# Pair 1's attention scores in a second buffer, half of their masking moved earlier, and four weight sums moved between engines

## The chip, the cores and the metric

The kernel runs on one core of a Trainium2 chip. The metric is the device time of one execution in microseconds (us). A core has five engines with a queue each: TensorE (PE; its weight loads are shown as PEld), VectorE (DVE), ScalarE (ACT), GpSimd (POOL) and SyncE (SP), which here only issues transfers (DMA).

## The reference

128 graphs of 128 nodes, with 512 features per node in fp32, go through two layers. Each layer's output is added to its input and normalised. Cut to what is computed:

```python
# layer 0: graph attention, 8 heads of 64 units
feats = einsum('bnf,hfu->bhnu', X, W)
dense = e_self[..., :, None] + e_neigh[..., None, :]   # two dot products per node and head
dense = leaky_relu(dense, 0.2) + -1e10 * (1 - A)
out   = softmax(dense) @ feats + b                      # heads side by side: 512 features
x = layernorm(x + relu(out))
# layer 1: two hypergraph convolutions over the same adjacency matrix
# conv(x) = D^-1 H B^-1 H^T (x @ W^T) + b
h = relu(conv(x; W1, b1))                               # 512 -> 1024
h = layer_norm(h) * gamma + beta
y = conv(h; W2, b2) + x                                 # 1024 -> 512
x = layernorm(x + y)
```

## The kernel before

**Pairs.** Two graphs are worked on together: 64 pairs, numbered p. A work step is a small function of a pair (for instance `masked`, line 586, which adds the mask to 128 x 512 scores on POOL). Each step has a lag and a time, and its due time is (p + lag) x T + time with T = 38.6. The list `todo` (lines 1140 to 1161) holds the steps done once, chiefly the preparation of the weights, with their due times; the dict `first` (lines 1163 to 1188) overrides due times for the first pairs, since the weights aren't ready then. At the end everything is sorted by due time and called in that order under a manual schedule. A due time is thus only a rank: it decides where in each engine's queue the instructions stand. Each engine runs its queue strictly in order, and semaphores make an instruction wait for its operands and for the buffer that it writes.

**Matrix products.** The large products use a scheme of seven half-size products in place of eight (numbers 1, 2, 6, 5, 7, 4, 3 in the order of issue). `chain` (line 326) makes the steps of one such product: seven products into PSUM banks named X, Y and W, and copies of X to SBUF by ACT between them. pf are the features of the attention, ph the products of the first convolution, py those of the second; pz is the product of y with the propagator R = D^-1 H B^-1 H^T. The scheme needs sums of blocks of the operands: `x_sums` (line 474, xS), `z_sums` (836, zS) and `h_sums` on POOL for the moving data, and sums of the weights, which are done once. For W1 they are s1 to s4, each 128 x 1024 elements (`prepare_hidden`, lines 243 to 249); for W2 t1 to t4 (`second_sums`, lines 222 to 226, by way of `prepare_output_block_sums`, 305). Before that, `prepare_output_blocks` (295) folds gamma into W2's blocks.

**Attention of a pair.** `features` by the chain pf, then f_sum (503) on DVE joins the products; `spread_rows` (537) transposes the node terms and writes them to DRAM (rd) by a DMA of SP, and `neighbours` (559) reads them back broadcast over all partitions into the tile nb, two DMAs of 512 KB, one for each graph of the pair. Then, for each graph g and half i of the heads: `masked` (586, POOL), `leaky` (593, ACT), `largest` (607, DVE, row maximum nm), `exponential` (616, ACT). `e_write` and `e_read` (621 to 634, SP) send the exponentials through DRAM, and `e_transpose` (636, DVE) turns blocks of them into eT, which `attend_pair` (692, PE) multiplies with the features. `add_bias` (741, POOL) adds the bias to the features, `residual` (751, DVE) adds x, `rstds` (764, POOL) takes the reciprocal root of the variance (rsa), ACT scales (line 796) to give y. The first pairs 0 and 1 get their features by plain products (L523).

**Other steps named here.** `edges` (412 to 429, DVE) makes the transposed incidence matrix hT and its degrees, `scale_edges` (431, DVE) divides by them; `x_transpose` (382, DVE) gives xT; `h_sum` (865, DVE), `relu` (876, ACT), `square` (890, ACT) and `squares` (902, POOL) make the hidden layer and its mean square; `skip` (803, DVE) adds y and bias into the output tile o. `mask` (376, POOL) makes the tile neg.

**Buffers.** Tiles are allocated from a pool by tag; the same tag is the same memory, and a new tile of the tag waits for the readers of the old one. nb has one buffer. The tag sq, of the same size, holds the squares of the hidden layer from pair 0's on, and before that a raw block of layer 0's weights; the tag xS also serves early temporaries.

Of the kernel before, what the change touches and what calls it, by code (L numbers as in the profile page):

```python
# [8 lines left out]
F32 = mybir.dt.float32  # L9
AF = mybir.ActivationFunctionType  # L10
# [10 lines left out]
def kernel(  # L21
# [45 lines left out]
    nc = tc.nc  # L67
    G, N, F = x.shape
    P = 128
    DH = w1t.shape[1]  # L70
    H = 8
    U = F // H
    KF = F // P
# [10 lines left out]
    work = ctx.enter_context(tc.tile_pool(name="work", bufs=1))  # L84
# [4 lines left out]
    def bank(name):  # L89
        return psum.tile([P, HALF], F32, tag="bank", name=name)  # L90
# [106 lines left out]
    w1_sb = const.tile([P, 7, KF // 2, HALF], F32, name="w1_sb")  # L197
    w1_21 = work.tile([P, KF // 2, HALF], F32, tag="h", name="w1_21")
# [6 lines left out]
    ident = const.tile([P, P], F32, name="ident")  # L205
# [5 lines left out]
    for i in range(2):  # L211
        t = const.tile([P, 2, H, UW + 1], F32, name=f"ft{i}")
# [37 lines left out]

    gbs = const.tile([P, KH, 2], F32, name="gbs")
    made = {}

    def prepare_vectors():
        t = bank("vecs_T")
        nc.tensor.transpose(t[:, :3 * KH], vec_rows, ident[:3 * KH, :3 * KH])
        nc.scalar.copy(vecs.rearrange("p v k -> p (v k)"), t[:, :3 * KH])
# [58 lines left out]
    def step(lag, time, since=0, until=PAIRS):  # L316

        def keep(fn):
            steps.append((lag, time, fn.__name__, range(since, until), fn, ()))
            return fn  # L320
        return keep
# [236 lines left out]

    @step(1, 27.0)
    def neighbours(p, s):  # L560
        s["nb"] = work.tile([P, 2, H * N], F32, tag="nb", name=f"nb_{p}")
        for g in range(2):
            dst, src, hs = s["nb"][:, g, :], s["rd"], slice((2 + g) * H, (3 + g) * H)
            if p == 0:
                src = src[hs].rearrange("h b j -> (h b j)")
            else:
                dst = dst.rearrange("p (b x) -> p b x", b=NB)
                src = src[:, hs, :].rearrange("b h j -> b (h j)")
            queue = nc.scalar if p == 0 and g == 1 else nc.sync
            queue.dma_start(dst, src.partition_broadcast(P))  # L570
# [553 lines left out]
    for t, fn, *args in (  # L1124
# [21 lines left out]
        (15.46, load_weights, (nc.sync, w1_blocks[:1:-1], w1t, F // 2, HALF)),  # L1146
        (16.1, everywhere, (b2_bc, b2, nc.sync)),
        (79.0, prepare_hidden, (nc.gpsimd, 0)), (79.1, prepare_hidden, (nc.gpsimd, 1)),
        (120.7, prepare_hidden, (nc.gpsimd, 2)), (110.6, prepare_hidden, (nc.vector, 3)),
        (15.5, prepare_output_vectors, ()), (16.0, prepare_output, ()),  # L1150
        (78.3, prepare_rows, ()), (78.79, prepare_output_sums, ()),
        (78.99, prepare_output_spread, (0, "gw")), (98.0, prepare_output_spread, (1, "bw")),
        (98.1, prepare_output_bias, ()), (98.2, prepare_output_blocks, (slice(0, 1),)),
        (99.75, prepare_output_blocks, (slice(1, 2),)),
        (117.8, prepare_output_blocks, (slice(2, 3),)),
        (118.1, prepare_output_blocks, (slice(3, 4),)),
        (126.5, prepare_output_block_sums, (nc.gpsimd, slice(0, 2))),
        (126.57, prepare_output_block_sums, (nc.vector, slice(2, 3))),
        (141.0, prepare_output_block_sums, (nc.vector, slice(3, 4))),
        (100.0, prepare_mean_columns, ()),  # L1160
    ]

    first = {
        ("spread_rows", 0): 13.5, ("neighbours", 0): 14.0,
        ("nodes", 0): 12.9, ("write_nodes", 0): 12.92, ("spread_nodes", 0): 15.9,
        ("edges", 0): 14.46, ("edges", 2): 119.2,
        ("x_transpose", 2, 0): 120.5, ("x_transpose", 2, 1): 121.1, ("scale_edges", 0): 14.47, ("propagator", 0): 14.55,
        ("r_evict", 0): 97.845,
        ("spread_rows", 1): 15.72, ("nodes", 1): 15.55, ("write_nodes", 1): 15.85,
        ("edges", 1): 110.4, ("scale_edges", 1): 110.5, ("neighbours", 1): 80.1,  # L1170
        ("propagator", 1): 121.7, ("spread_nodes", 1): 80.3, ("r_evict", 1): 121.8,
        ("leaky", 0, 1, 1): 77.65, ("leaky", 0, 0, 1): 73.6, ("largest", 0, 0, 1): 75.3,
        ("attend", 0, 0, 0): 78.95, ("attend", 0, 0, 1): 78.96, ("attend", 0, 1, 0): 78.97,
        ("attend", 0, 1, 1): 78.98, ("attended", 0, 0): 97.8, ("attended", 0, 1): 97.82,
        ("add_bias", 0, 0): 13.6, ("add_bias", 0, 1): 13.61,
        ("residual", 0, 0): 97.81, ("residual", 0, 1): 97.83, ("rstds", 0, "a"): 97.84,
        ("leaky", 1, 0, 0): 113.0, ("leaky", 1, 0, 1): 117.9, ("leaky", 1, 1, 0): 119.9,
        ("largest", 1, 0, 0): 113.1, ("largest", 1, 0, 1): 118.2, ("largest", 1, 1, 0): 120.2,
        ("masked", 1, 0, 0): 98.0, ("masked", 1, 0, 1): 98.1, ("masked", 1, 1, 0): 98.2, ("masked", 1, 1, 1): 120.65,
        ("exponential", 1, 0, 0): 119.85, ("exponential", 1, 1, 1): 126.6,  # L1180
        ("square", 0, 0, 0): 134.5, ("square", 0, 0, 1): 134.6,
        ("mask", 3): 152.0, ("sum_blocks", 0): 149.75, ("write_sums", 0): 149.76,
        ("read_sums", 0): 149.77,
# [96 lines left out]
```

## Time and profile before

| | |
|---|---|
| time, median of 3 runs (lowest to highest) | 2387.93 us (2385.42 to 2389.12) |
| the profiled execution's own time | 2389.21 us |
| its span from first to last instruction | 2387.4 us |
| granted TensorE clock, mean | 0.998 |
| PE busy | 2357.5 us, 99% |
| DVE busy | 2089.5 us, 88% |
| POOL busy | 1824.8 us, 76% |
| ACT busy | 1528.3 us, 64% |
| DMA | 347.09 MB, 145 GB/s over the span |

Durations below come from the profiled execution. A timeline row gives start and duration in us, engine, line, operation, output and inputs with their shapes, a count, and, in brackets, the idle time of the engine before it with what released it. "L249" is line 249 of the kernel. A row with a count of more than one covers adjacent instructions.

### The profile page before, as it was taken

The page shows a single profiled execution, that of the slowest core. Times are in us where ns is not written, and L with a number is a line of the kernel's source. Part 1 is how long each engine was busy: PE and PEld are TensorE (multiplying, and loading weights), DVE is VectorE, ACT ScalarE, POOL GpSimd, SP SyncE. Part 2 cuts the span into 40 slices and gives each one's busy share as a digit, 9 for nine tenths or more (in the row PEclk, how much of TensorE's full clock was granted, in tenths as well). Part 3 has the DMA queues.
Part 4 walks back from the last instruction along what each step waited for, and adds up shares of the span by engine and source line. Part 5 has one row for each costly group of instructions (what it writes and reads, how often), then busy time and mean ns, then how long its engine had stood idle before and what let it go on. Part 6 is the DMA issues. An engine that isn't in the chain of part 4 may idle for free.

```text
span 2387.4 us, 80667 instructions
## 1 busy us (share of the span) xinstructions
PE 2357.5 (99%) x32309; PEld 1941.2 (81%) x32309; DVE 2089.5 (88%) x4456; ACT 1528.3 (64%) x4481; POOL 1824.8 (76%) x2060
## 2 busy tenths in 40 slices
PE   7999999999999999999999999999999999999998
PEld 5777887878878888888888888888888887888886
DVE  7989888889898898898898988988988989889886
ACT  4565766766756667667667666666576676666763
POOL 5877787787777877877877878778778777787784
PEclk9999999999999999999999999999999999999999
DMA  6545555555545545455555545545555555455431
GB/s 198 137 144 147 150 150 137 154 150 143 155 144 149 149 149 145 148 150 150 142 148 153 148 142 156 150 144 144 148 148 149 147 141 149 144 148 152 146 118 50
DMA packets 431134, 347.09 MB, mean 145 GB/s; under 512 B 151440, under 2 KB 380328, under 8 KB 430760
## 3 DMA queue, kind: packets, MB, share of 16 engines
q1 hardware_dynamic: 427288, 337.46, 49.7%
q8 instruction: 256, 4.19, 0.7%
q10 hardware_dynamic: 3472, 4.47, 0.6%
q14 instruction: 118, 0.97, 0.2%
HBM read 239.08 MB, written 102.73 MB: 143 GB/s over the span
## 4 chain that ended last, share of the span: by engine, by line
PE 91%; DMA 3%; DVE 3%; ACT 1%; issue 1%; SPq 1%; POOL 0%; DVEq 0%; POOLq 0%; ACTq 0%
PE phX L97 18%; PE pyX L97 17%; PE phW L97 9%; PE pfX L97 9%; PE pyW L97 8%; PE phY L97 4%; PE pfW L97 4%; PE pq L97 4%; PE pav L705 4%; PE pz L97 4%; PE pyY L97 4%; PE pfY L97 2%; DMA nb<-rd 1%; PE pd L97 1%; DMA rd<-rows 1%; PE pf L523 1%
## 5 line engine op out<-in xcount | busy, mean ns | idle before, releaser
L344 ACT COPY py<-pyX 128x257 f32<-128x257 f32 x189 | 70.6, 374 | 529.3 <-PE pyX L97 445.6
L97 PEld LDWEIGHTS phX<-zS,w_sb 128*64 128x64 f32 x6144 | 347.7, 137 | 37.4 <-POOL ft L744 22.8
L97 PE MATMUL phX<-zS,w_sb 128*64 128x128 f32 x6144 | 370.7, 273 | 2.6 <-ACT ph L344 2.6
L906 POOL TENSOR_TENSOR sq<-sq 128x512 f32<-128x512 f32 (+2 forms) x384 | 343.2, 894 | 20.1
L589 POOL TENSOR_TENSOR nb<-nb,neg 128x512 f32<-128x512 f32 x256 | 319.8, 1281 | 29.5 <-DMA nb<-rd 26.5
L605 ACT ACTIVATE nb<-nb,ft 128x128 f32<-128x128 f32 x1020 | 325.1, 392 | 16.7 <-POOL nb L589 16.4
L619 ACT ACTIVATE nb<-nb,nm 128x128 f32<-128x128 f32 x1024 | 319.4, 391 | 4.7 <-DVE nm L611 4.7
L769 POOL TENSOR_TENSOR rso<-veo,mhalf 128x2 f32<-128x2 f32 x63 | 44.1, 700 | 337.4 <-DVE veo L767 337.4
L97 PE MATMUL pyX<-w_sb,h 128*64 128x257 f32 x2016 | 241.8, 379 | 0.5 <-ACT py L344 0.5
L97 PE MATMUL pyX<-w_sb,hS 128*64 128x257 f32 x2016 | 241.9, 379 | 0.0
L97 PE MATMUL pyW<-w_sb,hS 128*64 128x256 f32 x2016 | 241.2, 379 | 0.1
L883 ACT ACTIVATE h<-h,vecs 128x128 f32<-128x128 f32 x768 | 239.7, 393 | 1.9 <-DVE h L868 1.1
L611 DVE TENSOR_REDUCE nm<-nb 128x4 f32<-128x512 f32 x256 | 175.2, 684 | 50.5 <-ACT nb L605 42.2
L744 POOL TENSOR_TENSOR ft<-ft,b_bc 128x512 f32<-128x512 f32 x128 | 203.9, 1612 | 6.0 <-ACT ft L533 6.0
L97 PEld LDWEIGHTS pyX<-w_sb,h 128*64 128x64 f32 x2016 | 158.5, 136 | 61.4 <-ACT py L344 0.9
L97 PEld LDWEIGHTS pyW<-w_sb,hS 128*64 128x64 f32 x2016 | 158.1, 136 | 60.4 <-issue 0.7
L97 PEld LDWEIGHTS pyX<-w_sb,hS 128*64 128x64 f32 x2016 | 151.9, 136 | 53.1
L640 DVE STREAM_TRANSPOSE eT<-eb 128x512 f32<-128x512 f32 x252 | 163.5, 685 | 4.5 <-DMA eb<-ed 3.6
L807 DVE SCALAR_TENSOR_TENSOR o<-y,b_bc 128x512 f32<-128x512 f32 x128 | 166.7, 1341 | 0.0
L894 ACT ACTIVATE sq<-h 128x512 f32<-128x512 f32 x256 | 160.8, 629 | 2.1
L1008 DVE SCALAR_TENSOR_TENSOR y<-y,rsh,bw_bc 128x512 f32<-128x512 f32 x126 | 148.1, 1213 | 15.7 <-POOL rsh L1004 15.7
L469 POOL TENSOR_TENSOR hS<-h 128x512 f32<-128x512 f32 x126 | 161.8, 1284 | 0.0
(178 smaller groups left out, 5603.9 us busy)
## 6 DMA issues: line engine op xcount, KB each, us to landing
nb<-rd SPq DMA_DIRECT2D x127, 512.0 KB, 5.9
ed<-nb SPq DMA_DIRECT2D x126, 512.0 KB, 2.7
eb<-ed SPq DMA_DIRECT2D x504, 128.0 KB, 2.9
x<-in_x_dram SPq DMA_DIRECT2D x64, 512.0 KB, 4.1
out_dram<-o SPq DMA_DIRECT2D x63, 512.0 KB, 3.7
xb<-in_x_dram SPq DMA_DIRECT2D x248, 128.0 KB, 3.0
a<-in_adj_dram SPq DMA_DIRECT2D x64, 128.0 KB
w<-in_adj_dram SPq DMA_DIRECT2D x128, 64.0 KB, 4.0
```

The lines of the kernel that those rows point to most:

```text
L97: nc.tensor.matmul(to[rows], lhs[:, rows], rhs, start=start, stop=stop, skip_group_check=True)
L469: engine.tensor_tensor(t[:, i], in0, in1, op=op)
L589: nc.gpsimd.tensor_tensor(t, t, neg[:, :, None, :].to_broadcast([P, NB, HH, B]), op=ALU.add)
L605: nc.scalar.activation(t, t, AF.Prelu, bias=s["ft"][:, g, h, 0:1], alpha=SLOPE)
L611: nc.vector.tensor_reduce(s["nm"][:, g, hs], scores(p, s, g, hs).rearrange("p b h j -> p h b j"), AX.XY, ALU.max, negate=True,)
L619: nc.scalar.activation(t, t, AF.Exp, bias=s["nm"][:, g, h:h + 1])
L640: nc.vector.transpose(s["eT"][:, g, hs, :].rearrange("p h (b i) -> p h b i", b=NB), s["eb", g][:, :, hs, :].rearrange("p b h j -> p h b j"),)
L744: nc.gpsimd.tensor_tensor(t, t, b0_bc.rearrange("p (h u) -> p h u", h=H), op=ALU.add)
L807: nc.vector.scalar_tensor_tensor(s["o"][:, g, :], s["y"][:, g, :], 2.0, b2_bc, op0=ALU.mult, op1=ALU.add)
L883: nc.scalar.activation(dst[:, k, :], src[:, k, :], AF.Relu, bias=b1_sb[:, c:c + 1])
L894: nc.scalar.activation(s["sq"][:, g, q * KH // 2:(q + 1) * KH // 2, :], hid(s, g, q), AF.Square, scale=DH ** -0.5,)
L906: nc.gpsimd.tensor_tensor(t[:, :n, :], t[:, :n, :], t[:, n:2 * n, :], op=ALU.add)
```

## The change

Four things are changed, all in the first pairs and in the preparation of weights.

- The scores of pair 1 get a tile of the tag sq in place of nb, and the step `neighbours` of pair 1 is due at 16.15 and not 80.1: in SP's queue its two DMAs now stand ahead of loads for pair 2 (xb, a, w).
- `masked`, `leaky`, `largest` and `exponential` of pair 1 get new due times. Two of its four masks stand on POOL before the weight sum s2, the other two ahead of s4; the first two leaky steps stand on ACT before pair 0's y is scaled.
- The weight sum s3 = a11 - w1_21 leaves POOL: PE multiplies a11 by the identity and w1_21 by minus the identity into the same PSUM bank, for two blocks of 512 columns (four products of 128 x 512), and ACT copies the two banks to SBUF. s4, t3 and t4 leave DVE for POOL.
- Steps around them are reordered: edges(1), edges(2), x_transpose(2), e_transpose(1, 1) and the blocks of W2. From pair 3 on the order of every engine's instructions is unchanged.

```diff
--- before.py
+++ after.py
@@ -251,6 +251,21 @@
     gbs = const.tile([P, KH, 2], F32, name="gbs")
     made = {}
 
+    def prepare_minus():
+        made["minus"] = work.tile([P, P], F32, tag="xS", name="minus")
+        nc.scalar.activation(made["minus"], ident, AF.Identity, scale=-1.0)
+
+    def prepare_hidden_banks():
+        made["s3"] = [bank(f"s3_{k}") for k in range(KF // 2)]
+
+    def prepare_hidden_products():
+        for k, t in enumerate(made["s3"]):
+            nc.tensor.matmul(t, ident, w1_sb[:, 0, k, :], start=True, stop=False)
+            nc.tensor.matmul(t, made["minus"], w1_21[:, k, :], start=False, stop=True)
+
+    def prepare_hidden_out(k):
+        nc.scalar.copy(w1_sb[:, 5, k, :], made["s3"][k])
+
     def prepare_vectors():
         t = bank("vecs_T")
         nc.tensor.transpose(t[:, :3 * KH], vec_rows, ident[:3 * KH, :3 * KH])
@@ -558,7 +573,9 @@
 
     @step(1, 27.0)
     def neighbours(p, s):
-        s["nb"] = work.tile([P, 2, H * N], F32, tag="nb", name=f"nb_{p}")
+        s["nb"] = work.tile(
+            [P, 2, H * N], F32, tag="sq" if p == 1 else "nb", name=f"nb_{p}"
+        )
         for g in range(2):
             dst, src, hs = s["nb"][:, g, :], s["rd"], slice((2 + g) * H, (3 + g) * H)
             if p == 0:
@@ -1146,38 +1163,65 @@
         (15.46, load_weights, (nc.sync, w1_blocks[:1:-1], w1t, F // 2, HALF)),
         (16.1, everywhere, (b2_bc, b2, nc.sync)),
         (79.0, prepare_hidden, (nc.gpsimd, 0)), (79.1, prepare_hidden, (nc.gpsimd, 1)),
-        (120.7, prepare_hidden, (nc.gpsimd, 2)), (110.6, prepare_hidden, (nc.vector, 3)),
+        (98.2, prepare_hidden, (nc.gpsimd, 3)), (15.52, prepare_minus, ()),
+        (78.985, prepare_hidden_banks, ()), (98.05, prepare_hidden_products, ()),
+        (110.35, prepare_hidden_out, (0,)), (119.95, prepare_hidden_out, (1,)),
         (15.5, prepare_output_vectors, ()), (16.0, prepare_output, ()),
         (78.3, prepare_rows, ()), (78.79, prepare_output_sums, ()),
         (78.99, prepare_output_spread, (0, "gw")), (98.0, prepare_output_spread, (1, "bw")),
         (98.1, prepare_output_bias, ()), (98.2, prepare_output_blocks, (slice(0, 1),)),
-        (99.75, prepare_output_blocks, (slice(1, 2),)),
-        (117.8, prepare_output_blocks, (slice(2, 3),)),
-        (118.1, prepare_output_blocks, (slice(3, 4),)),
-        (126.5, prepare_output_block_sums, (nc.gpsimd, slice(0, 2))),
-        (126.57, prepare_output_block_sums, (nc.vector, slice(2, 3))),
-        (141.0, prepare_output_block_sums, (nc.vector, slice(3, 4))),
+        (98.25, prepare_output_blocks, (slice(1, 2),)),
+        (99.0, prepare_output_blocks, (slice(2, 3),)),
+        (99.1, prepare_output_blocks, (slice(3, 4),)),
+        (120.65, prepare_output_block_sums, (nc.gpsimd, slice(0, 1))),
+        (126.5, prepare_output_block_sums, (nc.gpsimd, slice(1, 2))),
+        (126.57, prepare_output_block_sums, (nc.gpsimd, slice(2, 3))),
+        (139.3, prepare_output_block_sums, (nc.gpsimd, slice(3, 4))),
         (100.0, prepare_mean_columns, ()),
     ]
 
     first = {
+        ("e_transpose", 1, 1, 1): 132.48,
+        ("e_transpose", 1, 1, 0): 132.47,
+        ("edges", 2): 126.58,
+        ("x_transpose", 2, 1): 117.95,
+        ("x_transpose", 2, 0): 117.9,
+        ("scale_edges", 1): 98.6,
+        ("edges", 1): 98.5,
+        ("exponential", 1, 1, 1): 126.52,
+        ("exponential", 1, 1, 0): 121.95,
+        ("exponential", 1, 0, 1): 119.9,
+        ("exponential", 1, 0, 0): 119.85,
+        ("largest", 1, 1, 1): 121.9,
+        ("largest", 1, 1, 0): 117.86,
+        ("largest", 1, 0, 1): 98.31,
+        ("largest", 1, 0, 0): 98.3,
+        ("leaky", 1, 1, 1): 121.8,
+        ("leaky", 1, 1, 0): 117.85,
+        ("leaky", 1, 0, 1): 79.08,
+        ("leaky", 1, 0, 0): 79.06,
+        ("masked", 1, 1, 1): 98.1,
+        ("masked", 1, 1, 0): 98.0,
+        ("masked", 1, 0, 1): 79.07,
+        ("masked", 1, 0, 0): 79.05,
+        ("neighbours", 1): 16.15,
         ("spread_rows", 0): 13.5, ("neighbours", 0): 14.0,
         ("nodes", 0): 12.9, ("write_nodes", 0): 12.92, ("spread_nodes", 0): 15.9,
-        ("edges", 0): 14.46, ("edges", 2): 119.2,
-        ("x_transpose", 2, 0): 120.5, ("x_transpose", 2, 1): 121.1, ("scale_edges", 0): 14.47, ("propagator", 0): 14.55,
+        ("edges", 0): 14.46, 
+        ("scale_edges", 0): 14.47, ("propagator", 0): 14.55,
         ("r_evict", 0): 97.845,
         ("spread_rows", 1): 15.72, ("nodes", 1): 15.55, ("write_nodes", 1): 15.85,
-        ("edges", 1): 110.4, ("scale_edges", 1): 110.5, ("neighbours", 1): 80.1,
+        
         ("propagator", 1): 121.7, ("spread_nodes", 1): 80.3, ("r_evict", 1): 121.8,
         ("leaky", 0, 1, 1): 77.65, ("leaky", 0, 0, 1): 73.6, ("largest", 0, 0, 1): 75.3,
         ("attend", 0, 0, 0): 78.95, ("attend", 0, 0, 1): 78.96, ("attend", 0, 1, 0): 78.97,
         ("attend", 0, 1, 1): 78.98, ("attended", 0, 0): 97.8, ("attended", 0, 1): 97.82,
         ("add_bias", 0, 0): 13.6, ("add_bias", 0, 1): 13.61,
         ("residual", 0, 0): 97.81, ("residual", 0, 1): 97.83, ("rstds", 0, "a"): 97.84,
-        ("leaky", 1, 0, 0): 113.0, ("leaky", 1, 0, 1): 117.9, ("leaky", 1, 1, 0): 119.9,
-        ("largest", 1, 0, 0): 113.1, ("largest", 1, 0, 1): 118.2, ("largest", 1, 1, 0): 120.2,
-        ("masked", 1, 0, 0): 98.0, ("masked", 1, 0, 1): 98.1, ("masked", 1, 1, 0): 98.2, ("masked", 1, 1, 1): 120.65,
-        ("exponential", 1, 0, 0): 119.85, ("exponential", 1, 1, 1): 126.6,
+        
+        
+        
+        
         ("square", 0, 0, 0): 134.5, ("square", 0, 0, 1): 134.6,
         ("mask", 3): 152.0, ("sum_blocks", 0): 149.75, ("write_sums", 0): 149.76,
         ("read_sums", 0): 149.77,
```

## The prediction

> **What bounds the kernel now.** First the page's busy shares, then a table of stretches, to see where PE stands idle:
>
> ```profile
> PE 2357.5 (99%) x32309; PEld 1941.2 (81%) x32309; DVE 2089.5 (88%) x4456; ACT 1528.3 (64%) x4481; POOL 1824.8 (76%) x2060
> ```
>
> Stretches (us; busy and count of PE, PEld, DVE, ACT, POOL; clock; DMA share; GB/s):
>
> ```profile
> 40.00:44.00 4.00, 3.16 (x30) 1.34 (x26) 3.76 (x10) 0.58 (x1) 0.92 (x1) 1.00 0.95 174
> 44.00:48.00 4.00, 0.57 (x6) 0.57 (x8) 3.90 (x12) 2.01 (x6) 2.55 (x3) 0.55 0.51 167
> 48.00:52.00 4.00, 4.00 (x48) 4.00 (x46) 3.90 (x13) 2.68 (x9) 2.50 (x7) 0.60 0.32 56
> 60.00:100.00 40.00, 34.98 (x479) 28.84 (x476) 38.83 (x74) 22.88 (x69) 34.80 (x35) 1.00 0.54 124
> 100.00:132.00 32.00, 29.77 (x376) 22.58 (x374) 28.14 (x63) 17.67 (x52) 21.95 (x22) 1.00 0.54 156
> 132.00:200.00 68.00, 68.00 (x946) 53.95 (x948) 60.38 (x129) 43.45 (x129) 52.20 (x61) 1.00 0.50 146
> 300.00:1000.00 700.00, 699.68 (x9700) 569.15 (x9698) 620.90 (x1328) 453.46 (x1333) 546.53 (x615) 1.00 0.52 148
> ```
>
> From 132 us PE is full; the change moves nothing there. So only the fill can pay. In it the timeline has these PE gaps: 4.27 before pz, 0.69, 0.26, 0.67 and 0.48 at 61 to 70, 0.92 at 90.54, 1.91 at 96.16, 0.34 at 116.22, 1.89 at 131.88: 11.4 us, 0.48% of the span, is all that closing gaps can win. To it comes a clock of 0.55 to 0.60 at 44 to 52, in which pz took 3.68 us where later ones take 1.75 to 1.94. Meanwhile DVE is 94 to 98% busy: in the fill it is the second bound.
>
> The timeline rows that the change touches (start, us, engine, line; the bracket is idle time before and its releaser):
>
> ```profile
> 36.11 2.37 POOL L249 TENSOR_TENSOR w_sb<-w,w_sb 128x1024 f32<-128x1024 f32 x1 [2.67 <-DMA w<-in_w1t_dram]
> 39.38 1.22 SPq L570 DMA_DIRECT2D nb<-rd  x2
> ...
> 45.45 0.71 POOL L769 TENSOR_TENSOR rsa<-vea,mhalf 128x2 f32<-128x2 f32 x1 [4.52 <-DVE vea L767]
> ...
> 47.43 3.68 PE L97 MATMUL pz<-R,y 128*64 128x128 f32 x32 [4.27 <-ACT y L796]
> ...
> 50.63 1.22 DVE L249 TENSOR_TENSOR w_sb<-w_sb 128x1024 f32<-128x1024 f32 x1
> ...
> 63.19 1.37 DVE L226 TENSOR_TENSOR w_sb<-w_sb,w 128x1024 f32<-128x1024 f32 x1
> ...
> 68.13 4.79 DVE L807 SCALAR_TENSOR_TENSOR o<-y,b_bc 128x512 f32<-128x512 f32 x2
> ...
> 75.58 2.15 DVE L226 TENSOR_TENSOR w_sb<-w_sb 128x1024 f32<-128x1024 f32 x1
> ...
> 96.16 1.97 PE L97 MATMUL phX<-zS,w_sb 128*64 128x128 f32 x32 [1.91 <-ACT ph L344]
> ```
>
> POOL stands idle for 4.52 us before rsa; three weight sums (1.22, 1.37, 2.15) sit in DVE's full queue. The chain of waits ends the fill with a transfer:
>
> ```profile
> 117.54 4.28 DMA rd<-rows
> 121.83 2.96 DMA nb<-rd
> 124.79 2.55 issue
> 131.88 1.97 PE phX L97 x32
> ```
>
> [...] 2.37 on POOL against 1.22 on DVE for one 128x1024 sum. [...] the two skips take 4.79 beside POOL's sums (L807's mean is 1.69 over the fill) and a residual (L753) 0.66 to 1.81. [...] the gaps of 1.9 halved nothing.
>
> **The change, part by part.** Sums are against the profiled execution: 2389.21 us with a span of 2387.4, 1.8 around it, 1.3 above the median of 2387.93.
>
> *Second buffer and early load.* Pair 1's scores waited for pair 0's nb, read by PE's transposes until 38.7. In a tile tagged sq they wait for rd's write, landed at 36.3. The two nb DMAs now stand before xb x4, a and w x2 of pair 2 on SP; those seven issue after the wait, 3 us later, and serve work at 51 us and beyond: nothing. The load itself: issue 36.3, landing 3.0 later (nb at 121.83 in the chain) to 6.2 (230.67 there, busier queues), so 39.3 to 42.5; I take 41, as the DMA share is 0.98 at 36 to 40.
>
> *POOL.* After s1 (ends 38.48) it runs two masks (1.28 each), s2 (2.37), and then rsa: 2.56 + 2.37 = 4.93, ending at 45.9 with the landing at 41. That is about when y needs rsa, since y is late too: its two residuals (0.90 and 0.69 at 40.57 and 43.52) had POOL mostly idle and now run beside masks. L753's spread, 0.66 to 1.81, bounds it at 0.0 to 1.1 each; I take 1.1 together, so pz begins at 48.5 instead of 47.43. Behind rsa stand two more masks and s4, 2.56 + 2.37 from 46.6, then the memsets and neg (0.6): zS starts at 52.1 where it started at 51.83. The phX that reads it, at 54.45, is where it was, perhaps 0.3 late. t1 takes the place of s3 at 55.94 (2.37 both within 0.3), t2 and t3 stand where t1 and t2 stood; so t4 is what POOL gains. It comes before the squares at 78.83, and POOL has no gap from 61.25 to 91: its 2.2 to 2.7 would push rsa at 84.77 and pz at 87.24, had not xS and hS come earlier by about as much (xT, which xS waited 2.94 for, is moved ahead of edges(2), 2.4 us). Nothing; cover gone, up to 2.4 on pz.
>
> *PE.* s3 becomes four 128x512 products in the gap before pz. No row has that shape; two passes of 2x512 took 1.12 (gw), so 0.56 each at the least; the 128x264 product of L523 takes 0.45, so 0.87 for 512. I take 0.87: 3.5 in a gap of 4.27, so they end at 46.7. Operands late, they would push pz one for one, up to 3.5. PE is then idle for 1.8 and not 4.27 before pz, so the clock stays full: pz takes 1.85 and not 3.68. pz's end: 48.5 + 1.85 = 50.35 against 51.11; the next phX is at about 50.4 against 50.90, -0.5 (bounds -1.7 with unhindered residuals, +1.3 if the clock halves all the same). But at 54.45 zS decides, as worked out under POOL: of the -0.5 **0.0** is left (up to +0.3). ACT's two copies (0.58 each) and minus (0.39) fall in its idle time at 39.3 to 43.2 and in queues that PE doesn't wait for until 61: nothing, up to 0.6 on the gap at 61.09.
>
> *DVE up to 74.* s4 (1.22) and t3 (1.37) leave. edges(2), with its degree 2.4 us in all, moves from 56.09 to about 62, behind an h_sum, and its scale_edges follows: 2.4 - 1.37 = +1.0 before the h_sum of (1,0) at 66.31, 1.9 if the small DVE operations there, now beside add_bias and t2, wait once more. Its relus hold up the pf copy: pfX at 70.22 comes +1.0 to +1.9, I take **+1.4**. Then eT(1,1) twice (1.29) precedes the skips and the f_sum that frees pfW at 73.76; pfW is already 1.4 late by pfX, and the skips and f_sum have that much slack from it: nothing more (bounds 0 to 1.3).
>
> *DVE from 75 to 100.* t4 is gone: -2.15 at 75.58 on a full DVE, which feeds rden, y and the largest of pair 2: 1.4 - 2.15 = -0.75 there, which the gap of 0.92 can take, and the gap of 1.91, which waits on ACT behind an exp and DVE's largest, as well. At 100: **-1.0** (bounds -2.8, both gaps, to +1.4, neither).
>
> *The last gap.* rd's issue at 117.54 follows the rows transposed at 117.09 and SP's own ab issues (to 117.44); 4.28 + 2.96 + 2.55 behind it don't shrink. The rows come after pair 2's products and would be earlier by 1.0, SP's queue, with its own waits for DMAs and POOL, only in part: a third is kept. Sum at 132: **-0.3** (-2.8 to +1.7). 2387.93 - 0.3 = 2387.6.
>
> **Rivals.** A, the gaps close: 0.69 + 0.26 + 0.67 + 0.48 = 2.1 and 0.92 + 1.91 = 2.83 are won, and rd starts as much earlier. With 0.5 kept from pz, -5.4: 2382.5. For it: DVE loses 4.74 us in a stretch where it is the bound. Against: edges and eT move into the very stretch, and the last gap takes back. B, slower: nb lands late. POOL stands at the first mask, and s2, rsa, y and pz stand behind it. Free until 41 to 41.5; from there one for one. If it lands at 45.9, as its second half did before, rsa is at 45.9 + 4.93 = 50.8, +5.4, pz runs at half clock again, of which no later step has to give back more than the 0.3 of the forecast: +5.1, 2393. For it: a DMA share of 0.95 to 0.98 at 36 to 44; against: 3 us earlier issue, ahead of xb. C, no win from the clock or t4: s3 leaves PE idle enough that pz runs at half rate, phX +1.3, and DVE's +1.4 at 70 isn't given back, as t4 on POOL holds up rsa: +1 to +2, 2389.5. D, it is all hidden: the transfer at 117.54 starts when it did, 2387.9, inside the forecast.
>
> **How the numbers follow.** Forecast with D, 0.71 (own range 2385.5 to 2389.7); C 0.12; A 0.10; B 0.07. A change under 0.2% (4.8 us) is about what can't be told from none here: three runs spread over 3.7. Faster takes most of A: 0.09; slower takes B and a tail of C: 0.08; same 0.83. The range leaves out B and most of A: 2384.0 to 2390.8.
>
> **What would show it.** nb landing and POOL's first L589 of pair 1 at 41 or sooner; four short PE rows between 43 and 47; clock 1.00 at 44 to 52 and pz near 1.85; rsa within 1 us of 45.5; pfX at 71 and pfW at 74 to 75; the gaps at 90 and 96 smaller; PE's phX after the last gap near 131.6 and the same busy PE afterwards. Wrong if POOL waits for nb past 42, if pz stays at 3.68, or if anything after 132 has changed.

## The result and the profile after

| | before | after |
|---|---|---|
| time, median of 20 runs each (lowest to highest) | 2387.91 us (2385.29 to 2389.94) | 2391.31 us (2388.61 to 2393.98) |
| ratio to before, 95% interval | | 1.0015 (1.0008 to 1.0022) |
| span of the profiled execution | 2387.4 us | 2390.7 us |
| third pair's first phX (the "last gap" ends) | 131.88 us | 135.55 us |
| the next 20 pairs | 729.33 us | 731.31 us |
| the 41 pairs after those | 1488.60 us | 1486.28 us |

Slower by 3.4 us. The last three rows come from the starts of phX in the two traces, one execution each. They show two losses: 3.7 us in the fill and 2.0 in pairs whose instructions the change doesn't touch. (The 2.3 that after wins at the end is a disturbance at 1938 to 1957 us in the profiled execution of before, with PE gaps of 0.62 and 1.26.) Such rows compare kernels only roughly: the runs of one kernel spread over 5 us or so, and one early product (pf of pair 0's second graph) starts anywhere from 19.9 to 21.5 us in the fourteen traces, 1.1 us earlier in after than in before.

The table of stretches, after (us; busy and count of PE, PEld, DVE, ACT, POOL; clock; DMA share; GB/s):

```profile
40.00:44.00 4.00, 4.00 (x8) 1.53 (x9) 3.79 (x9) 1.00 (x4) 2.30 (x2) 0.78 1.01 197
44.00:48.00 4.00, 3.73 (x7) 1.25 (x5) 3.93 (x12) 2.45 (x9) 4.00 (x4) 0.79 1.05 142
48.00:52.00 4.00, 3.08 (x56) 3.03 (x58) 3.90 (x10) 3.69 (x8) 4.00 (x3) 1.00 0.45 81
60.00:100.00 40.00, 33.30 (x412) 26.78 (x410) 30.26 (x68) 19.98 (x59) 30.98 (x30) 0.91 0.43 106
100.00:132.00 32.00, 31.92 (x418) 24.93 (x416) 29.14 (x67) 16.99 (x49) 21.55 (x23) 1.00 0.60 156
```

The clock is full where pz runs now, as intended, but it is at 0.91 in 60 to 100, where it was 1.00, and DVE is busy for 30.26 of those 40 us where it was busy for 38.83. The timeline shows where both come from:

```profile
66.91 1.73 SPq L648 DMA_DIRECT2D eb<-ed  x4
...
71.55 1.30 DVE L657 STREAM_TRANSPOSE eT<-eb 128x512 f32<-128x512 f32 x2 [3.16 <-DMA eb<-ed]
...
72.78 4.33 DVE L824 SCALAR_TENSOR_TENSOR o<-y,b_bc 128x512 f32<-128x512 f32 x2
...
77.03 0.42 DVE L524 TENSOR_TENSOR ft<-pf,pfW 128x264 f32<-128x264 f32 x1
...
77.59 2.02 PE L97 MATMUL pfW<-w_sb,xS 128*64 128x264 f32 x8 [3.92 <-DVE ft L524]
...
79.37 3.71 PE L722 MATMUL pav<-ft,eT 128*64 128x65 f32 x64
```

DVE reaches the two turns eT of pair 1's second graph at 68.4 and stands there for 3.16 us, because the last of eb lands at 71.5. The skips, the f_sum and with it PE's pfW are behind it. In the kernel before, the two skips filled that time, so that eT, at 73.52, waited for nothing:

```profile
67.65 1.73 SPq L631 DMA_DIRECT2D eb<-ed  x4
...
73.52 1.29 DVE L640 STREAM_TRANSPOSE eT<-eb 128x512 f32<-128x512 f32 x2
73.76 1.09 PE L97 MATMUL pfW<-w_sb,xS 128*64 128x264 f32 x8
...
74.65 2.06 PE L705 MATMUL pav<-ft,eT 128*64 128x65 f32 x64
```

PE's gap of 3.92 also costs clock, granted at half from 76.37 to 83.20 us: pfW takes 2.02 (1.09 before) and pav 3.71 (2.06). PE is 6.3 us late at the next pyX (82.84 against 76.52). The gaps of 0.92 and 1.91 at 90 and 96, now 0 and 0.50, give 2.3 of that back, so that 3.7 is left at the end of the fill.

### The profile page after: what moved, and what is told of

Read it like the earlier page. It is cut to its first block, busy times and chain, and to the rows that moved or that the text cites. A ratio compares the mean times of both kernels' runs of the same rounds, so it can differ in the third digit from the quotient of the medians.

```text
span 2390.7 us, 80690 instructions
## 1 busy us (share of the span) xinstructions
PE 2362.5 (99%) x32317; PEld 1942.0 (81%) x32317; DVE 2084.3 (87%) x4453; ACT 1530.0 (64%) x4484; POOL 1827.9 (76%) x2062
## 3 DMA queue, kind: packets, MB, share of 16 engines
q8 instruction: 256, 4.19, 0.7%
## 4 chain that ended last, share of the span: by engine, by line
PE 92%; DMA 3%; DVE 1%; ACT 1%; POOL 1%; issue 1%; SPq 0%; POOLq 0%; DVEq 0%; ACTq 0%
PE phX L97 18%; PE pyX L97 17%; PE phW L97 9%; PE pfX L97 9%; PE pyW L97 8%; PE pfW L97 5%; PE phY L97 5%; PE pq L97 5%; PE pav L722 4%; PE pyY L97 4%; PE pz L97 4%; PE pfY L97 2%; DMA nb<-rd 2%; DMA rd<-rows 1%; PE pd L97 1%; PE pf L538 1%
```

## Experiments

Each ratio is against runs of the kernel before on the same chip and has its 95% interval. "Fill" is the start of the third pair's first phX, "pairs" the 20 pairs after it. A rd is called held where SP issues nb more than 2.2 us after rd (nb waits for rd's landing), counted over the last 60 pairs, which are numbered from 0 here. A trace is one execution of some twenty: a median and a trace need not agree.

### The turns, the skips and t4

**E1: eT back behind the skips.**

```diff
     first = {
-        ("e_transpose", 1, 1, 1): 132.48,
-        ("e_transpose", 1, 1, 0): 132.47,
```

> The changed kernel, but with the two turns eT of pair 1's second graph (e_transpose 1, 1) behind the skips and the two f_sums again, where they stood before; nothing else is touched. Theory T (a wait at the head of DVE's queue: eT stands idle for 3.2 us until eb lands at 71.5, and the skips and the f_sum that frees pfW stand behind it): the gap of 3.9 before pfW goes to under 0.5, the pav after it takes 2.1 and not 3.7, and the time falls by 4 to 5.5, to 2386 to 2387.5. Rival S (the skips are slow because the sum t4 now runs on POOL beside them): skips of 4.3 stay and the f_sum is late by 1 to 2 us all the same; 2389 to 2390. Rival M (the loss comes from the moved masks, nb and s3 before 60 us): no gain, 2391.

Measured: 2392.0 us, 1.0013 (1.0007 to 1.0020). In the trace the stall is gone as expected: pfW starts at 73.97, pav takes 2.06. The time isn't: theory T missed. The fill ends at 131.71, but in the gap of 2.07 at its end the clock falls to half (phX 3.30 and phY 2.30 in place of 1.97 and 1.92), and the pairs take 733.6, 1.7 of it for that clock and 2.3 in three gaps at 536, 646 and 793 us. So E1 removes one loss and shows two that don't come from eT. Lines of E1's trace, and of E11's, the same kernel once more:

```profile
131.71 3.30 PE L97 MATMUL phX<-zT,w_sb 128*64 128x128 f32 x32 [2.07 <-ACT zT L848]
```

```profile
131.10 1.97 PE L97 MATMUL phX<-zT,w_sb 128*64 128x128 f32 x32 [2.08 <-ACT zT L848]
```

**E3: eT alone**, added to the kernel before (the two lines above, with + for -).

> The kernel before, with only this one part of the change: the two turns eT of pair 1's second graph moved ahead of pair 0's skips. Theory T: eb of that graph lands at 72 or later there, so DVE idles for 3 to 4 us at 68, skips and f_sum follow, pfW comes near 78 with a gap of 4 and the clock at half for some 7 us: slower by 3 to 4.5, 2391 to 2392.5. Rivals S and M: the kernel before has neither t4 on POOL nor the moved masks, so under 1 us.

Measured: 2393.6 us, 1.0020 (1.0014 to 1.0027), +4.8 us. Timeline of E3:

```profile
71.76 1.30 DVE L640 STREAM_TRANSPOSE eT<-eb 128x512 f32<-128x512 f32 x2 [3.91 <-DMA eb<-ed]
72.99 2.32 DVE L807 SCALAR_TENSOR_TENSOR o<-y,b_bc 128x512 f32<-128x512 f32 x2
...
75.80 1.85 PE L97 MATMUL pfW<-w_sb,xS 128*64 128x264 f32 x8 [2.17 <-DVE ft L509]
...
77.37 3.03 PE L705 MATMUL pav<-ft,eT 128*64 128x65 f32 x64
```

The wait, the late pfW and the clock are all there without any other part of the change; the fill ends at 135.41 and the pairs take 729.4, as before. That eT's place alone is enough for such a loss of the fill is shown, in the trace and in the time.

**E4: t4 back on DVE** at its old due time, in the changed kernel.

```diff
-        (139.3, prepare_output_block_sums, (nc.gpsimd, slice(3, 4))),
+        (141.0, prepare_output_block_sums, (nc.vector, slice(3, 4))),
```

> The changed kernel, with t4 alone back on DVE at its old place. Theory T: the wait for eb and the skips behind it are untouched, though the skips lose a POOL partner (4.3 to perhaps 3.0), and DVE has t4's 1.4 to 2.2 more after the f_sums: 2390 to 2392. Rival S: the skips shorten to under 2 us, pfW comes near 75 and the time near 2388.5.

Measured: 2393.3 us, 1.0017 (1.0009 to 1.0025), no gain. The skips shorten from 4.33 to 2.65, yet eT waits 3.75 us, pfW comes at 76.77 after a gap of 2.83, and pav takes 3.64. Rival S falls: beside t4 the skips took 1.7 longer, but t4 does not make the stall.

**E2: skips behind the f_sums**, eT left in front.

```diff
-        ... ("skip", 0): 132.5,
+        ... ("skip", 0): 137.3,
```

> The changed kernel, with eT left in front, but pair 0's two skips moved behind the two f_sums. Theory T: eT still waits for eb until about 71.5, then the f_sum starts at once, near 72.9, and pfW near 73.6, without a gap: the wait alone costs PE nothing, what costs is the 4.3 us of skips that are pushed out behind it. The skips now stand before the last f_sum, rows and rd of pair 2, which come up to 3 us later than in the kernel before; 2387 to 2390. If the wait itself costs (nothing to do with the skips), pfW stays at 77.6 and the time at 2391.

Measured: 2391.6 us, 1.0013 (1.0006 to 1.0019), a miss: that is the time expected if the wait itself costs. In its trace eT waits 2.17 for eb, the f_sum starts at 73.92, 3.1 us earlier than in after, and PE no longer waits for it. But pfW still comes only at 77.28, because PE lost its time earlier: pfX at 72 waited 2.35 us for hS of POOL, and the clock was at half from 73.1 to 76.6. The last gap is 3.92, again with the clock at half after it. What made these two gaps stays open, and this trace is of the slowest of the 21 runs (2397.35). So E2 does not decide whether the wait costs only through the skips behind it.

### Why untouched pairs are slower

The two traces differ in single pairs. In pair 13 of the 60 SP issues rd and nb so, in before and after:

```profile
629.57 0.33 SPq L552 DMA_DIRECT2D rd<-rows  x1
631.06 1.68 SPq L570 DMA_DIRECT2D nb<-rd  x2
```

```profile
633.05 0.33 SPq L567 DMA_DIRECT2D rd<-rows  x1
636.71 0.92 SPq L587 DMA_DIRECT2D nb<-rd  x2
```

1.49 us from rd to nb in one and 3.66 in the other; nb's landing, POOL's masks, ACT's leaky and zT follow. In these two traces PE waits 0.2 to 1.26 us at phX in the seven of the 60 pairs each where the first mask starts 9.25 to 10.09 us after rd (10.09 and 1.04 here), and not by over 0.2 in any other. Most held rd stay below that; it takes a long transfer of nb besides (6.37 us from issue to landing here). The trace's view of DMA for 633.3 to 635.5 us in after names what else runs:

```profile
DMA packets 145, 0.03 MB, mean 15 GB/s; under 512 B 144, under 2 KB 144, under 8 KB 144
## 3 DMA queue, kind: packets, MB, share of 16 engines
q1 hardware_dynamic: 144, 0.02, 5.5%
q8 instruction: 1, 0.02, 3.7%
```

One packet of kind "instruction", 16 KB. It starts 0.88 us after rd's issue and takes 1.30, so it ends at 2.18. Of rd's 128 packets 120 have started by 1.03 us; the other eight start at 2.16 to 2.30, as the fetch ends (one engine's share is an estimate: 128 packets over the 16 engines of the view). In before's pair 13 all 128 have started by 1.04. Over the fourteen traces, 318 of 840 rd are held; in 312 of these the last packets of rd start later than 1.3 us, and in only 4 of the other 522. In each of after's pairs 0 to 17 the late packets begin within 0.03 us of the fetch's end; how it holds them up isn't shown. It is not the whole delay: nb's issue follows rd's last packet by about 1.0 us where rd is held and by 0.39 where it is free, and what the difference comes from isn't shown.

There are 256 such packets, 4.19 MB, four a pair. That they carry PE's instructions is an estimate from the profile's counts (about 65 bytes for each of the 64,618 PE rows of before), which E5, E7 to E10 and E12 below bear out: rows added on PE move them. From pair to pair the fetch moves slowly against rd: in before it starts at 0.63 us after rd in pair 0, and from pair 12 on at 1.26 or later, where nearly every rd is free. (The start alone doesn't decide it: after's pairs 10 and 15 are held with fetches at 1.26 and 1.37.) s3 adds 16 PE rows (32317 products and as many loads, for 32309), which is 16/1010 of a pair of 36.4 us, an estimate of 0.6 us: after fetches at 0.55, 0.47 and 0.87 where before does at 0.84, 1.00 and 1.27 (pairs 3, 6 and 9), and rd is held up to pair 17. Held are 14 rd in before (pairs 0 to 9 and four later), 21 in after (0 to 17 and three later).

**E5: 16 PE rows alone**, 8 transposes of the identity whose result is overwritten, added to the kernel before where PE waits for x. E7 to E10 and E12 have the same edit with another count.

```diff
         s["px"] = [bank(f"px_{p}_{g}") for g in range(2)]
+        for _ in range(8 if p == 0 else 0):
+            nc.tensor.transpose(s["px"][0][:, :24], ident[:24, :], ident[:24, :24])
```

> The kernel before, with nothing of the change, but with 8 small transposes of the identity added on PE in its idle 8 us at the start (8 weight loads and 8 products: 16 PE instructions, as many as the change's s3 adds). Theory F (instruction fetches): PE's instructions come in blocks of 16 KB by DMA, four a pair; one of them runs 0.6 to 1.3 us after rd's issue [...]. Sixteen more PE instructions put every later fetch about 0.5 us earlier in the pair, so it hits rd until some pair 17 to 21 and no longer until 10 to 15: the waits of POOL for nb and small PE gaps in the first 20 pairs, together 1.5 to 2.5 us, so 2390 to 2391.5. Rival (the moved nb load, the masks or the sums of the change cause the later loss): no difference from the kernel before, 2388.7 within 0.6.

Measured: 2388.8 us, 1.0006 (0.9997 to 1.0014). 20 rd are held, pairs 0 to 17, 19 and 34, much as in the changed kernel and unlike before; the pairs take 730.1, +0.8. That the rows move the fetch onto rd is shown, the loss in the pairs came out at half of what was expected, and the time alone doesn't tell it from nothing. The fill of this trace, without any other part of the change, ends at 134.27, 2.4 later than before, with the clock at half in 41.6 to 45.0 and 48.4 to 55.3; whether the rows have to do with that isn't shown.

**E6: s3 back on POOL**, in E1's kernel: minus, the banks, the products and the copies out, and

```diff
-        (98.2, prepare_hidden, (nc.gpsimd, 3)), (15.52, prepare_minus, ()),
+        (98.2, prepare_hidden, (nc.gpsimd, 3)), (120.7, prepare_hidden, (nc.gpsimd, 2)),
```

> The changed kernel with eT of pair 1's second graph behind the skips again (as in the first experiment), and s3 back on POOL as one sum: the four products, minus and the two copies are gone, PE has as many instructions as before. Theory F: rd is hit only in the first 10 to 15 pairs after the fill, as in the kernel before, and the fill is as in the first experiment, perhaps 1 us later for POOL's 2.4: 2388 to 2389.5, against 2392.0 of the first experiment. Rival (nb's move or the sums cause the later loss): 2391 to 2392.

Measured: 2390.6 us, 1.0015 (1.0009 to 1.0022). Only 15 rd are held, nearly the same ones as in before, but the time is a miss, in the fill and in the pairs. Timeline of E6:

```profile
46.76 0.71 POOL L786 TENSOR_TENSOR rsa<-vea,mhalf 128x2 f32<-128x2 f32 x1
...
48.74 3.68 PE L97 MATMUL pz<-R,y 128*64 128x128 f32 x32 [5.61 <-ACT y L813]
...
52.21 3.11 PE L97 MATMUL phX<-zT,w_sb 128*64 128x128 f32 x32
```

Without s3's products PE idles 5.61 us before pz and runs it and the next product at half clock: phY starts at 55.15, in after at 52.49. The fill ends at 134.25. So s3 on PE is worth about 2.6 us at phY between these two traces, through the clock, as the prediction had it. The 20 pairs take 731.1, as long as in after, though no PE row is added: PE waits 0.40 and 1.23 us at phX in pairs 1 and 4, which are held in before too and cost PE nothing there. Hence the length of the 20 pairs in one trace doesn't price the 16 rows; a table further down counts the pairs that differ.

**E7: 128 PE rows** in the kernel before. **E8: 112** in E1's, 128 with s3's.

> The kernel before, with 64 such transposes (128 PE instructions) in PE's idle time at the start. Theory F: the fetches fall some 4.5 us earlier in the pair, so none hits rd: from the first pair nb is issued 1.4 us after rd and not 3, POOL's wait for nb goes, and the gaps before phX of 0.3 to 1.3 with it. Faster by 1 to 2.5 us, 2386 to 2387.5. The clock may also be full earlier than at 13.7 us, which the fill hides. Rival (the fetch is no cause): no difference, or slower if the transposes last past 8.2 us.

> The changed kernel with eT behind the skips, and 56 such transposes at the start (with s3's 16 it has 128 PE instructions more than before). Theory F: the fill of the first experiment, 0.2 to 0.4 better than before at 132 us, and no fetch on rd: 2385.5 to 2387.5, better than both kernels. Rival: 2391 to 2392, as the first experiment.

Measured: E7 2387.3 us, 1.0001 (0.9992 to 1.0009); E8 2386.9 us, 0.9998 (0.9990 to 1.0007). Waits of POOL in E7 (engine, line, releaser: us, times, longest), 140 to 860 us; in before that row reads 14.3, 16, 1.7:

```profile
POOL nb L591 <- DMA nb<-rd: 5.8, 8, 1.5
```

In the first 40 pairs only pairs 6, 9, 20 and 34 are held in E7; its 20 pairs take 727.8 and E8's 727.4, 1.5 to 1.9 less than before, and PE waits at phX for 0.1 us in all. Only 0.7 us of the difference is PE's waiting in before; the rest stands in PE's busy time (728.6 in before, 727.7 and 727.4 in these) and isn't explained. In time neither is clear of before, a miss of the expected gain. The drift brings the fetch onto rd in pairs 41 to 59, and E7's fill ends at 133.31: ACT's issue of the first two rd transfers, at about 21 us, took 2.32 in E7 and 2.36 in E8, 0.84 before, so the copy of xT behind it and PE's pf came late (pf waits 1.58 us for xT in E8). A fetch runs at that time in both (from 20.45 and 21.18), but E12 below shows an issue of 2.14 with its fetch only at 24.28, so the cause of that stays open. E8 is level with before, and 3 to 4 us faster than the first run of the same kernel without the rows; against its second run, E11 below, the two aren't clear of each other.

**E9, E10, E12: 64 PE rows more than before**, in the kernel before, in E1's and in the changed kernel as it is; **E11: E1's kernel again.**

> The kernel before, with 32 small transposes (64 PE instructions) in PE's idle time at the start. With 128 the fetches left rd alone in the first 40 pairs (rd's write 1.4 us), [...]. Theory F: 64 put the fetch some 2.3 us earlier, at -1.7 to -0.9 from rd's issue, so rd is free in the first 20 pairs, which take 727.5 to 728 us and not 729.3[...]: faster by 1 to 2 us. Rival: the first 20 pairs take 729 or more and nb is issued 3 us after rd, as before.

> The changed kernel with eT behind the skips and 24 such transposes (with s3's 16 it has 64 PE instructions more than before). Theory F with T: no fetch on rd in the first 20 pairs and no stall of DVE at eT: 1 to 3 us faster than the kernel before. If fetches are no cause: 3 us slower than it, as the same kernel without the transposes.

> The changed kernel with eT behind the skips, once more, to stand beside the others of this group on one chip. From its first run: 3 us slower than the kernel before, rd held up in the first 18 pairs; whether the clock is at half at 132 us again is open (it was, for 3.4 us, after a gap of 2.1): if it is not, the fill's end is within 0.5 us of before and the loss is the pairs' 2 to 2.5 us.

> The changed kernel as it is (eT in front of the skips), with 24 such transposes. Theory F with T: the stall at eT stays (pfW near 77.6, the clock at half after it), +3.5 at 132 us, and the first 20 pairs take 727.5 to 728: 1.5 to 2.5 us slower than the kernel before, some 3 to 4 slower than the same without the stall. If the stall at eT is without consequence: as the kernel without it.

| | ratio (interval) | fill | 20 pairs | next 41 | held |
|---|---|---|---|---|---|
| E9 | 1.0013 (1.0007 to 1.0020) | 132.43 | 728.2 | 1489.5 | 35 |
| E10 | 1.0012 (1.0006 to 1.0019) | 130.86 | 729.6 | 1492.0 | 34 |
| E11 | 1.0005 (0.9997 to 1.0014) | 131.10 | 730.1 | 1486.3 | 21 |
| E12 | 1.0016 (1.0010 to 1.0023) | 134.44 | 729.9 | 1490.1 | 34 |

The gain expected of 64 rows is a miss: the fetch starts at -0.5 us from rd in the first pairs, drifts to 0.4 by pair 9 and stays on rd until pair 42. More than twice as many rd are held, and the pairs after the first 20 take 3 to 6 us longer than the 1486.3 of kernels whose fetch has gone by. The count of held rd follows the PE rows alone in all fourteen traces: 14 and 15 with none added (before, E3, E6), 20 to 22 with 16, 34 and 35 with 64, 21 and 25 with 128, wherever eT, t4 and s3 stand. What they cost shows best in pairs 10 to 19, which are nearly all free without added rows:

| PE rows added | traces | held in pairs 10 to 19 | PE's wait at phX there, us |
|---|---|---|---|
| none | before, E3, E6 | 1, 2, 1 | 0.0, 0.2, 0.0 |
| 16 | after, E1, E2, E4, E5, E11 | 8, 8, 9, 9, 9, 8 | 2.1, 2.3, 2.9, 2.4, 1.2, 0.7 |
| 64 | E9, E10, E12 | 10, 8, 9 | 0.4, 1.7, 0.5 |
| 128 | E7, E8 | 0, 1 | 0.1, 0.0 |

E12 against E10 is once more eT in front of the skips against eT behind them. The fills end 3.6 us apart, but the medians, 2391.2 and 2390.7, only 0.5, where 3 to 4 was expected: a miss.

E11 against E1 is one kernel twice: this time the clock stays full at the last gap (2.08) and the fill ends 0.8 before that of before. The two intervals overlap only at 1.0007 to 1.0014: one kernel, 2 us apart.

## Why the prediction was wrong

It forecast 2387.6 and no measurable change; 2391.3 was measured. Step by step:

- *Second buffer, masks, rsa*: right. The first mask starts at 41.70 (41 forecast), rsa at 46.93 (45.9), pz at 48.92 (48.5). Rival B did not come about.
- *s3 on PE, clock at pz*: right in effect. Clock full, pz 1.97 (1.85), phX at 50.71 (50.4); phX after zS at 54.48, so nothing was left of it, as worked out under POOL. The products took 0.94 each at full clock (0.87 forecast) but the first two 1.8 each, since the clock was at half from 42.2 to 45.7.
- *DVE up to 74*: **the step that failed.** It added the 1.29 us of the two turns and found them hidden in slack. The turns' input was not looked up: ed issued at 64.04 and eb at 67.65 to 69.4 in the trace of before, so eb would hardly land before 70 or so, and DVE would stand at it. The pieces behind it were named (skips, f_sum, pfW) and not priced after the wait: 3.16 + 1.30 + 4.33, against the 4.79 + 0 of before. pfW came at 77.59, +3.8 against before, where +1.4 for the other moves and "nothing more (bounds 0 to 1.3)" for eT were forecast; the clock added 2.5, which no bound held. The +1.4 did not come either: pfX, 70.22 before, starts at 69.93.
- *DVE from 75 to 100, the last gap*: once eT is back, the sum comes out: the fills of E1 and E11 end 0.2 and 0.8 before that of before (0.3 forecast), and the last gap, 2.07 for 1.89, takes back a part. In part that is luck. The +1.4 at pfX was 0.2 (70.43 and 70.39), and the gap of 0.92 closes while that of 1.91 stays at 1.79. A bound was also misread: the residuals (L753) take 0.66 to 1.23 in the fill, and 1.81 is the time of two skips (L807 at 101.23); nothing hung on it.
- *"From 132 us PE is full; the change moves nothing there"*: **the second step that failed.** The order is the same, but with 16 PE rows added in the fill the instruction fetches run 0.29 to 0.53 us earlier against rd in pairs 3, 6 and 9, and the chain from rd to zT, with little slack left, turns that into gaps. In pairs 10 to 19 PE waits 2.1 us at phX in after and not at all in before; the other traces with 16 rows have 0.7 to 2.9 there, those without 0.0 to 0.2.

Fill and pairs together are 5.6 in this trace, the medians 3.4 apart; the trace of before has its disturbance of 2.3 at the end. Both losses are shown in the traces. Open is how the 3.4 of the medians divides between them: eT alone costs 4.8 (E3), yet putting it back wins only 0.5 to 2.4 us (E1, E11, and E10 against E12), none of it clear of noise. A part of that may be the clock, since whether a gap of 2 us halves it differs from run to run, as E1 and E11 show. The fills of the traces fall in line with eT, 134.4 to 136.3 with it in front and 130.9 to 133.3 with it behind, but for E5 and E6 with 134.3. No version tried is clearly faster than the kernel before; the best, E8, equals it.

## What to carry to other kernels

Before an instruction is moved forward in an in-order queue, look up when its last input lands in the trace of before; that it waits for nothing there may only mean that its engine was late, and what is queued behind it inherits the wait (3.16 us at eT in after). A later stage with identical order is not thereby untouched: where a small transfer of every period sits on a chain with little slack, a handful of instructions added much earlier on the engine with the most instructions moved the instruction fetches against that transfer here (16 PE rows, by 0.29 to 0.53 us in three pairs), so compare its issue-to-landing time period by period. A PE gap is priced with the clock after it, as a chance and not as a certainty: one of 2.07 us cost 1.7 more in E1, one of 2.08 nothing in E11, and those of 1.91 in before and 2.09 in after left the clock full.

## What the runs showed of the hardware

- A 16 KB packet of kind "instruction" mostly takes 0.9 to 1.4 us, in before and in after. Where it overlapped rd in pair 13, eight of rd's 128 packets started late (2.16 to 2.30 us after the issue in after, in place of 1.04 at the latest in before). nb, which waits for rd's landing, was issued 2.2 to 3.7 us after rd in the held pairs of before and after, and mostly 1.42 in the others.
- The clock can fall while PE is busy. In after it was at half from 42.24 to 45.65 us, and 38.8 to 42.2 us show PE without a gap; what ran there was pav, gw and bw (products with 2 output rows) and two transposes. All periods at half clock between 14 and 2380 us, in all fourteen traces, lasted 3.41, 6.83 or 10.24 us (44.41 to 51.23 in before; 42.24 to 45.65 and 76.37 to 83.20 in after). Whether the light use is the reason, no run tested.
